# Layer 1 of a four-layer graph network: the order of TensorE's instructions written out by hand, with the next pair's features and the half's end as steps inside it

## The chip, the cores and the metric

The kernel runs on one core of one Trainium2 chip. The metric is the device time of one execution in microseconds (us), smaller is better. Most executions of one kernel agree within 0.3%.

## The reference

x has the shape (8, 2048, 64); adj is a 2048 x 2048 matrix of zeros and ones. Four layers follow each other, each as `x = x + layer(relu(layernorm(x)))`. The change lies in layer 1, a graph attention:

```python
h = jnp.matmul(input, W)
s_src = jnp.matmul(h, a[:C, 0])
s_dst = jnp.matmul(h, a[C:, 0])
e = jax.nn.leaky_relu(s_src[:, :, None] + s_dst[:, None, :], negative_slope=0.2)
attention = jax.nn.softmax(jnp.where(adj > 0.5, e, NEG_INF), axis=2)
return jax.nn.elu(jnp.matmul(attention, h))
```

Layer 0 is a hypergraph attention with a gate, layer 2 three rounds of a product with adj and two small linear maps, layer 3 a graph convolution of order 3 whose weights depend on the node.

## The kernel before

**Tiling.** Batches are taken in pairs: NP = 4 pairs, each with 2 x 64 features on the 128 partitions and N = 2048 nodes along the free axis. All of adj (transposed, 16 tiles `aT[m]` of 128 x 2048) lies in SBUF from the end of layer 0 on.

**Layer 1** is the class `Layer1`. For each pair p there is first a part that prepares the nodes as neighbours, `neighbour_steps(p)`, a generator. It goes through four chunks c of 512 columns. For each it loads x from DRAM on SP's queue, normalizes (`norm_steps`, lines 714 to 727: a matmul for the mean, L719; a subtraction on VectorE, L720; a square on ScalarE, L721; a matmul for the variance, L724; Ln and Exp on ScalarE, L725 and L726; the product on VectorE, L727), and then, twice, makes features of 256 nodes: four matmuls into `ph` (L1302; two in the text, each of them two records in the trace), an Exp `vd` on ScalarE (L1303), a copy `sc` (L1304) and a product `hS` (L1305) on VectorE. At the end come two small Exps `wd` and `rs` (L1311, L1313), a transpose `pr` (L1315), its copy `rr` and a store of that row to DRAM. It yields at some places, and the caller decides what is placed between. `mean` and `var` share one bank of PSUM (tag `ln`), and `ph` has one (tag `h`).

Then `attend` runs twice per pair, once for each half `hf` of the columns (1024 of them). It loads `R`, two broadcast rows of scores (512 KB each, three buffers in rotation), and loops over the 16 tiles m of neighbours:

- on VectorE two instructions `pt` (L1370), one for each batch of the pair, make the weights of 128 neighbours x 1024 nodes; there are five `pt` buffers;
- on TensorE `features` (L1355) adds `hS` times `pt` into `o`: four matmuls in column tiles of 64, so that the two batches can run beside each other;
- on TensorE `sums` (L1361) adds `vd` times `pt` into `dn`: four matmuls in column tiles of 32. `dn` has one buffer, `o` two.

For even m features come first, for odd m sums, so that equal kinds of two tiles m stand next to each other.

After the loop comes the half's end: `ds` takes `dn` out of PSUM (L1377), two matmuls `prd` spread it over the partitions (L1381), ScalarE takes Ln and Exp (L1382, L1383), and VectorE makes the product `res` (L1385), a minimum (L1387), after an Exp on ScalarE (L1388) the ELU (L1389) and the sum with x (L1390). POOL's queue stores it as x2 in DRAM (L1391).

**What sets the order.** The text gives each instruction a priority, its place. A planner then plays the program through with its own idea of costs and, on each engine, takes the first instruction in the text's order that it thinks is ready. So the instructions of an engine may be sent in another order than the text's; within the engine's queue they then run in that order. `tc.keep_in_program_order(ins)` binds one instruction to its place in the text. Before, it is used in layer 0's end, for one table load, and in layer 3; nothing in layer 1's loop is bound. In the text, `run` calls `attend(p, 0)`, then all of `neighbours(p + 1)`, then `attend(p, 1)`.

Pair 0's neighbours are made during the end of layer 0: `layer0` takes the steps of the same generator, two for each (p, c) of its last loop from the eighth on (`next(next_, None)`), and what is left after that loop. There, R of the first half is not loaded but made by 16 matmuls `pb` (L1326) and four copies on ScalarE (L1327).

Of the kernel before, what the change touches and what calls it, by code (L numbers as in the profile page):

```python
# [8 lines left out]
FP = mybir.dt.float32  # L9
FR = mybir.dt.float32r  # L10
AF = mybir.ActivationFunctionType
OP = mybir.AluOpType
# [4 lines left out]
P = 128  # L17
B, N, F = 8, 2048, 64
E = 64
NP = B // 2  # L20
NT = N // P
# [596 lines left out]
HN = N // 2  # L618
# [3 lines left out]
class Kit:  # L622


    def __init__(self, tc, t, pool):
        nc = self.nc = tc.nc
        self.tc, self.t = tc, t
        self.ident = pool.tile([P, P], FP, name="ident_f")
        make_identity(nc, self.ident)
        self.ones = pool.tile([P, F], FP, name="ones_f")  # L630
        nc.vector.memset(self.ones, 1.0)
        self.avg = pool.tile([P, P], FP, name="avg_f")
        nc.vector.memset(self.avg, 0.0)
        for b2 in range(2):
            nc.vector.memset(self.avg[half(b2), half(b2)], 1.0 / F)
        self.eps = pool.tile([P, 1], FP, name="eps_f")
        nc.vector.memset(self.eps, EPS)

        self.wide = pool.tile([P, P], FP, name="wide")
        nc.vector.memset(self.wide, 0.0)  # L640
        for q in range(4):
            nc.vector.memset(self.wide[32 * q : 32 * q + 32, half(q % 2)], 1.0 / 32)
        self.W1x = pool.tile([P, P + 4], FP, name="W1x")
        for k in ("W1v", "W1e", "W2", "Wvc", "Wec", "cb"):
            setattr(self, k, pool.tile([P, P], FP, name=f"{k}_f"))
        for k in ("b1", "b2c", "ivc", "b1c"):
            setattr(self, k, pool.tile([P, 1], FP, name=f"{k}_f"))

        self.bad = pool.tile([P, 7 + NT * NCW], FP, name="bad")
        nc.vector.memset(self.bad, 0.0)  # L650
# [35 lines left out]
    def layer2_weights(self, pool, ps):  # L686
# [21 lines left out]
        mm(pw, r, self.W1e, start=True, stop=True)  # L708
        nc.vector.tensor_copy(self.cb, pw)

    def use_ln_exp(self):
        self.tc.keep_in_program_order(self.nc.scalar.preload_act_table_set(LN_EXP))

    def norm_steps(self, dst, src, mean, var, xc, q):

        nc, mm = self.nc, self.nc.tensor.matmul
        n = dst.shape[-1] // CW
        for c in range(n):
            mm(mean[:, cols(c)], self.avg, src[:, cols(c)], start=True, stop=True)  # L719
        nc.vector.tensor_sub(xc, src, mean)  # L720
        nc.scalar.activation(q, xc, AF.Square)  # L721
        yield
        for c in range(n):
            mm(var[:, cols(c)], self.avg, q[:, cols(c)], start=True, stop=True)  # L724
        nc.scalar.activation(q, var, AF.Ln, bias=self.eps)  # L725
        nc.scalar.activation(q, q, AF.Exp, scale=-0.5)  # L726
        nc.vector.scalar_tensor_tensor(dst, xc, 0.0, q, op0=OP.max, op1=OP.mult)  # L727
        yield
# [525 lines left out]
class Layer1:  # L1254
# [14 lines left out]
        self.R = l1.enter_context(tc.tile_pool(name="l1_R", bufs=2, side="right", reuse_waits="tile"))  # L1269
        self.ps = ps = l1.enter_context(tc.tile_pool(name="l1_ps", bufs=1, space=PSUM, reuse_waits="tile"))  # L1270

    def neighbours(self, p):

        return [r for r in self.neighbour_steps(p)][-1]

    def neighbour_steps(self, p):


        kit, sb, ps, Wx = self.kit, self.sb, self.ps, self.kit.W1x
        tc, nc = kit.tc, kit.nc  # L1280
        mm = nc.tensor.matmul
        x1_dram, r_dram = self.x1_dram, self.r_dram
        hS = (self.sb2 if p % 2 else sb).tile([P, NT, P], FP, tag="hS", name="hS", bufs=1)
        vd = sb.tile([P, NT, 2], FP, tag="vd", name="vd")
        sc = sb.tile([P, NT, 4], FP, tag="sc", name="sc", bufs=1)
        wd = sb.tile([P, NT, 2], FP, tag="wd", name="wd")
        for c in range(NCW):
            x = sb.tile([P, CW], FP, tag="x", name="x1", bufs=1)
            nc.sync.dma_start(out=x, in_=x1_dram[p, :, cols(c)])
            mean = ps.tile([P, CW], FP, tag="ln", name="mean")  # L1290
            var = ps.tile([P, CW], FP, tag="ln", name="var")
            xc = sb.tile([P, CW], FP, tag="xc", name="xc")
            q = sb.tile([P, CW], FP, tag="q", name="q", bufs=1)
            hn = xc
            for _ in kit.norm_steps(hn, x, mean, var, xc, q):
                yield
            for g in range(2):
                ms = slice(4 * c + 2 * g, 4 * c + 2 * g + 2)
                ph = ps.tile([P, 2, P + 4], FP, tag="h", name="ph")
                for k in range(2):  # L1300
                    j = 2 * g + k
                    mm(ph[:, k, :], hn[:, j * P : (j + 1) * P], Wx, start=True, stop=True)  # L1302
                nc.scalar.activation(vd[:, ms, :], ph[:, :, P : P + 2], AF.Exp, scale=0.2)  # L1303
                nc.vector.tensor_copy(sc[:, ms, :], ph[:, :, P:])  # L1304
                nc.vector.tensor_tensor(  # L1305
                    hS[:, ms, :].rearrange("p t (b f) -> p t b f", b=2),
                    ph[:, :, 0:P].rearrange("p t (b f) -> p t b f", b=2),
                    vd[:, ms, :, None].to_broadcast([P, 2, 2, F]), op=OP.mult,
                )
        yield  # L1310
        nc.scalar.activation(wd, sc[:, :, 0:2], AF.Exp, scale=0.8)  # L1311
        rs = sb.tile([P, 2, NT], FP, tag="rs", name="rs", bufs=1)
        nc.scalar.activation(rs, sc[:, :, 2:4].rearrange("p t b -> p b t"), AF.Exp, scale=-0.8)  # L1313
        pr = ps.tile([2 * NT, P], FP, tag="h", name="pr")
        nc.tensor.transpose(pr, rs.rearrange("p b t -> p (b t)"), kit.ident)  # L1315
        rr = sb.tile([2 * NT, P], FP, tag="rr", name="rr", bufs=1)
        nc.vector.tensor_copy(rr, pr)
        nc.sync.dma_start(out=r_dram[p].rearrange("b (t n) -> (b t) n", n=P), in_=rr)
        self.first = [self.scores(p, 0, b2) for b2 in range(2)] if p == 0 else None

        for b2, r in enumerate(self.first or ()):
            for k in range(2):
                pb = ps.tile([P, 4, P], FP, tag=("ln", "h")[k], name="pb1")
                for j in range(4):
                    one = rs[:, b2, 4 * k + j : 4 * k + j + 1]
                    mm(pb[:, j, :], one.to_broadcast([P, P]), kit.ident, start=True, stop=True)  # L1326
                nc.scalar.copy(r[:, cols(k)], pb.rearrange("p k n -> p (k n)"))  # L1327
        yield hS, vd, wd
# [7 lines left out]
        self.kit.nc.sync.dma_start(out=r, in_=self.r_dram[p, b2 : b2 + 1, cols(hf, HN)].to_broadcast([P, HN]))  # L1336
        return r

    def attend(self, aT, p, hS, vd, wd, hf):
        kit, sb, ps, wide = self.kit, self.sb2, self.ps2, self.kit.wide  # L1340
        tc, nc = kit.tc, kit.nc
        mm = nc.tensor.matmul
        x1_dram, x2_dram, r_dram = self.x1_dram, self.x2_dram, self.r_dram
        s = cols(hf, HN)
        R = self.first or [self.scores(p, hf, b2) for b2 in range(2)]
        self.first = None
        x = sb.tile([P, HN], FP, tag="xr", name="xr", bufs=1)
        nc.sync.dma_start(out=x, in_=x1_dram[p, :, s])
        o = ps.tile([P, HN], FP, tag="o", name="o")
        dn = ps.tile([P, CW], FP, tag="dn", name="dn", bufs=1)  # L1350

# [14 lines left out]
        for m in range(NT):  # L1366
            pts = []
            for b2 in range(2):
# [2 lines left out]
                    pt, R[b2], wd[:, m, b2 : b2 + 1], aT[m][:, s].bitcast(FP), op0=OP.max, op1=OP.mult  # L1371
                )
                pts.append(pt)
            for f in (features, sums)[:: -1 if m % 2 else 1]:
                f(m, pts)
        ds = self.sb.tile([P, CW], FP, tag="xc", name="ds")
        nc.vector.tensor_scalar_max(ds, dn, 1e-30)  # L1377
        den = sb.tile([P, HN], FP, tag="den", name="den", bufs=1)
        for k in range(2):
            pr = ps.tile([P, CW], FP, tag="r", name="prd", bufs=1)  # L1380
            mm(pr, wide[half(k), :], ds[half(k), :], start=True, stop=True)  # L1381
            nc.scalar.activation(den[:, cols(k)], pr, AF.Ln)  # L1382
        nc.scalar.activation(den, den, AF.Exp, scale=-1.0)  # L1383
        r = sb.tile([P, HN], FP, tag="res", name="res", bufs=1)
        nc.vector.tensor_mul(r, o, den)  # L1385
        e = sb.tile([P, HN], FP, tag="den", name="e", bufs=1)
        nc.vector.tensor_scalar(e, r, 0.0, None, op0=OP.min)  # L1387
        nc.scalar.activation(e, e, AF.Exp)  # L1388
        nc.vector.scalar_tensor_tensor(e, e, -1.0, r, op0=OP.add, op1=OP.max)  # L1389
        nc.vector.tensor_add(x, x, e)  # L1390
        nc.gpsimd.dma_start(out=x2_dram[p, :, s], in_=x)  # L1391

    def run(self, aT, now):

        kit, l1 = self.kit, self.l1
        tc, nc = kit.tc, kit.nc
        self.pt = l1.enter_context(tc.tile_pool(name="att_pt", bufs=5, reuse_waits="tile"))
        self.sb2 = sb = l1.enter_context(tc.tile_pool(name="att_sb", bufs=2, reuse_waits="tile"))
        self.ps2 = l1.enter_context(tc.tile_pool(name="att_ps", bufs=2, space=PSUM, reuse_waits="tile"))
        kit.use_ln_exp()  # L1400
        for p in range(NP):
            self.attend(aT, p, *now, 0)
            if p + 1 < NP:
                after = self.neighbours(p + 1)
            self.attend(aT, p, *now, 1)
            now = after
        l1.close()


# [282 lines left out]
```

The softmax here doesn't subtract the row's maximum and nothing guards it: scores larger than these inputs give would overflow.

## Time and profile before

| what | value |
|---|---|
| device time, median of 3 runs | 2194.04 us (2191.21 to 2198.37) |
| the profiled run | 2193.25 us, its span 2191.5 us |
| busy in the span: PE, PEld, DVE, ACT, POOL | 2095.4, 1156.9, 1217.6, 452.3, 298.8 us |
| layer 1, first `o` to last `dn`/`o` | about 538 to 991 us |
| in it: `o` L1355, 1024 records | 267.7 us busy |
| in it: `dn` L1361, 1024 records | 142.4 us busy |
| in it: `pt` L1370, 256 instructions | 319.1 us busy |
| one `pt` (128 x 1024) | 1280 ns, 1.22 us from start to start |
| one Exp on 128 x 1024 (L1388) | 1058 ns |

PE is TensorE's matmuls, PEld its weight loads, DVE is VectorE, ACT is ScalarE, POOL is GpSimd; SP issues DMAs. In a timeline, instructions of one kind that follow each other are one row: the start, the length, engine, line, operation, what is written from what, and after the x how many. For the price of such a group in a full queue the text takes the time from its start to the start of the next row, since the modelled lengths overlap a little.

### The profile page before, as it was taken

How to read it: one execution, taken by the hardware profiler on the slowest of the kernel's cores; microseconds unless marked ns; L12 is line 12 of the kernel's file. 1: busy time of each engine (PE TensorE's matmuls, PEld its weight loads, DVE VectorE, ACT ScalarE, POOL GpSimd, SP SyncE). 2: the span in 40 equal slices, each digit the busy share in tenths (PEclk: the TensorE clock that was granted, in tenths of full speed). 3: DMA queues.
4: the chain of work that ended last, by engine and by line, in shares of the span. 5: the costliest groups of instructions: out<-in, count | busy, mean ns of one | idle time of the engine just before them, and what ended most of it. 6: DMA issues, size and time to landing. Idle time of an engine off the chain costs nothing.

```text
span 2191.5 us, 23784 instructions
## 1 busy us (share of the span) xinstructions
PE 2095.4 (96%) x9164; PEld 1156.9 (53%) x9164; DVE 1217.6 (56%) x1890; ACT 452.3 (21%) x852; POOL 298.8 (14%) x416
## 2 busy tenths in 40 slices
PE   7999999888999999998999999999999999999997
PEld 4777656523222222225666546774557664576653
DVE  6575488867888787884223563116551236501265
ACT  4312244465111102002121111120111211112100
POOL 0211154401000000000110121101111011111022
PEclk9999799989999999999999999999999999999999
DMA  5665362155011101104210014000030100101000
GB/s 123 195 199 158 105 220 50 40 168 164 29 49 34 62 30 44 39 30 132 68 43 8 22 33 127 24 20 19 25 101 6 44 10 21 42 1 34 12 19 12
DMA packets 86154, 140.26 MB, mean 64 GB/s; under 512 B 33040, under 2 KB 33296, under 8 KB 83792
## 3 DMA queue, kind: packets, MB, share of 16 engines
q1 hardware_dynamic: 67984, 88.05, 13.7%
q0 software_dynamic: 18048, 50.60, 7.7%
q8 instruction: 74, 1.21, 0.2%
q14 instruction: 48, 0.39, 0.1%
HBM read 107.89 MB, written 30.74 MB: 63 GB/s over the span
## 4 chain that ended last, share of the span: by engine, by line
PE 63%; issue 16%; DVE 7%; DMA 5%; POOL 4%; ACT 3%; POOLq 0%; DVEq 0%; SPq 0%; ACTq 0%
PE acc L1486 19%; PE o L1355 11%; PE u L1564 7%; PE dn L1361 6%; DMA raw<-in_adjT 3%; PE acc L913 2%; PE var L724 2%; PE pgs L1141 2%; PE py L1459 2%; PE mean L719 2%; PE acc L1515 1%; DVE ex L1139 1%; DMA at<-in_adjT 1%; POOL fold L1583 1%; PE ph L1302 1%
## 5 line engine op out<-in xcount | busy, mean ns | idle before, releaser
L1486 PE MATMUL acc<-aT,hi 128*128 128x512 f32 x960 | 401.2, 418 | 0.0
L1486 PE MATMUL acc<-aT,lo 128*128 128x512 f32 x960 | 388.2, 405 | 0.0
L1355 PE MATMUL o<-pt,hS 128*64 128x512 f32 x1024 | 267.7, 605 | 5.8 <-DVE pt L1370 5.8
L1370 DVE SCALAR_TENSOR_TENSOR pt<-R,wd,aT 128x1024 f32<-128x1024 f32 x192 | 239.1, 1280 | 38.6 <-PE dn L1361 21.6
L1564 PE MATMUL u<-W3f,y 64*128 64x512 f32 x1024 | 258.2, 592 | 0.0
L1572 DVE TENSOR_TENSOR pr<-u,embf 128x512 f32<-128x512 f32 x256 | 171.4, 687 | 123.0 <-PE u L1564 111.0
L1486 PEld LDWEIGHTS acc<-aT,hi 128*128 128x128 f32 x960 | 180.6, 188 | 61.8 <-issue 23.2
L1486 PEld LDWEIGHTS acc<-aT,lo 128*128 128x128 f32 x960 | 180.7, 188 | 51.2 <-issue 13.6
L1564 PEld LDWEIGHTS u<-W3f,y 64*128 64x128 f32 x1024 | 104.1, 187 | 124.8 <-issue 124.8
L1355 PEld LDWEIGHTS o<-pt,hS 128*64 128x64 f32 x1024 | 70.5, 137 | 187.1 <-issue 173.5
L1564 PE MATMUL u<-W3f,v 64*128 64x512 f32 x512 | 146.4, 617 | 0.0
L1361 PE MATMUL dn<-pt,vd 128*32 128x512 f32 x1024 | 142.4, 599 | 0.0
L913 PE MATMUL acc<-at,Y 128*128 128x512 f32 x512 | 137.4, 414 | 2.3 <-DVE ev L922 2.3
L1486 PE MATMUL acc<-aTl,lo 128*128 128x512 f32 x320 | 127.6, 399 | 5.6 <-DVE lo L1463 3.9
L1486 PE MATMUL acc<-aTl,hi 128*128 128x512 f32 x320 | 126.9, 397 | 4.7 <-ACT hi L1467 4.7
L1583 POOL TENSOR_TENSOR fold<-fold 128x256 f32<-128x256 f32 x64 | 47.6, 743 | 555.9 <-DVE fold L1582 555.9
L913 PEld LDWEIGHTS acc<-at,Y 128*128 128x128 f32 x512 | 95.9, 196 | 26.5 <-issue 4.9
L1466 DVE TENSOR_TENSOR yb<-py,cb_f 128x512 f32<-128x512 f32 x32 | 22.1, 690 | 156.1 <-PE py L1459 156.1
L721 ACT ACTIVATE q<-xc 128x512 f32<-128x512 f32 (+1 forms) x56 | 38.7, 691 | 264.8 <-DVE xc L720 253.4
L1576 DVE TENSOR_TENSOR pr<-pr 128x512 f32<-128x512 f32 x128 | 88.1, 688 | 2.2
L1442 DVE SCALAR_TENSOR_TENSOR raw<-raw 128x512 f32<-128x512 f32 x64 | 47.8, 750 | 72.4 <-DMA raw<-in_adjT 72.1
L1479 DVE TENSOR_TENSOR lo<-tp,hi 128x512 fp32r<-128x512 f32 x32 | 22.2, 692 | 117.5 <-ACT hi L1478 117.5
(278 smaller groups left out, 2717.7 us busy)
## 6 DMA issues: line engine op xcount, KB each, us to landing
at<-in_adjT POOLq DMA_DIRECT2D x32, 512.0 KB, 4.6
raw<-in_adjT SPq DMA_DIRECT2D x64, 256.0 KB, 3.3
aT<-in_adjT POOLq DMA_DIRECT2D x12, 1024.0 KB, 6.4
R<-r_dram SPq DMA_DIRECT2D x14, 512.0 KB, 3.6
hi_dram<-hi SPq DMA_DIRECT2D x16, 264.0 KB, 2.5
lo_dram<-lo SPq DMA_DIRECT2D x16, 264.0 KB, 3.6
hhi<-hi_dram POOLq DMA_DIRECT2D x16, 264.0 KB, 3.1
hlo<-lo_dram POOLq DMA_DIRECT2D x16, 264.0 KB, 3.1
```

What stands on the lines that cost most here:

```text
L719: mm(mean[:, cols(c)], self.avg, src[:, cols(c)], start=True, stop=True)
L724: mm(var[:, cols(c)], self.avg, q[:, cols(c)], start=True, stop=True)
L913: mm(acc[p], Y[h][:, m, p, :], at[:, k, :], start=m + h == 0, stop=m == NT - 1 and h == 1)
L1355: mm(o[half(b2), cols(k)], hS[:, m, half(b2)], pts[b2][:, cols(k)], start=m == 0, stop=m == NT - 1)
L1361: mm(dn[q : q + 32, :], vd[:, m, b2 : b2 + 1].to_broadcast([P, 32]), pts[b2][:, cols(k)], start=m == 0, stop=m == NT - 1, tile_position=(0 ...
L1370: nc.vector.scalar_tensor_tensor(pt, R[b2], wd[:, m, b2 : b2 + 1], aT[m][:, s].bitcast(FP), op0=OP.max, op1=OP.mult)
L1442: nc.vector.scalar_tensor_tensor(a, a, 0.5, a, op0=OP.is_gt, op1=OP.not_equal, accum_out=kit.bad[:, k : k + 1])
L1486: mm(acc, part[:, m % 4, :], aT[m][:, cols(c)], start=start, stop=m == NT - 1 and part is y[m // 4][1])
L1564: one = mm(u[h].rearrange("p d o -> p (d o)"), src[half(h), :], W3[half(h), kk, cols(w)], start=kk == 0, stop=kk == 2,)
L1572: nc.vector.tensor_tensor(a, u[h], emb[:, i, 8 * w : 8 * w + 8, None].to_broadcast([P, 8, F]), op=OP.mult)
L1576: nc.vector.tensor_add(pr[h], pr[h], a)
L1583: nc.gpsimd.tensor_add(fold[:, :, 0:2, :], fold[:, :, 0:2, :], fold[:, :, 2:4, :])
```

## The change

- A switch `kit.strict`, on from the start of layer 1's `run` to its end. While it is on, every matmul of `features`, `sums`, the totals `prd`, the norms and `ph`, and the transpose `pr`, is bound to its place in the text (`Kit.mm`).
- `attend` calls `between(m)` between the first and the second of features and sums of each m. There, in `run`, the next pair's neighbour steps are taken, by a pattern of (2, 0, 1, 0, 1) steps over five m, one fewer at m = 0 and 20, with m counted over both halves (0 to 31). So they begin at m = 0 of the first half and the 17th and last is taken at m = 22.
- The generator yields more often: after the mean, after the variance, and after each of the two feature groups, so 17 steps instead of 10 up to the result.
- The half's end is cut into two functions that run in the next half, after the first of features and sums: the first total `prd` at m = 1, the second and all that follows it at m = 2. Only `ds` stays at the end of its own half. After the last half both run at once.
- The minimum on VectorE (L1387) becomes a Relu with scale -1 on ScalarE, and the Exp after it gets the scale -1.

```diff
+    def mm(self, *args, **kw):
+        one = self.nc.tensor.matmul(*args, **kw)
+        if self.strict:
+            self.tc.keep_in_program_order(one)
...
     def norm_steps(self, dst, src, mean, var, xc, q):
-        nc, mm = self.nc, self.nc.tensor.matmul
+        nc, mm = self.nc, self.mm
...
     def neighbour_steps(self, p):
-        mm = nc.tensor.matmul
+        nc, mm = kit.nc, kit.mm
...
             for g in range(2):
+                if g:
+                    yield
                 ms = slice(4 * c + 2 * g, 4 * c + 2 * g + 2)
...
-        yield
+            yield
         nc.scalar.activation(wd, sc[:, :, 0:2], AF.Exp, scale=0.8)
...
-        nc.tensor.transpose(pr, rs.rearrange("p b t -> p (b t)"), kit.ident)
+        one = nc.tensor.transpose(pr, rs.rearrange("p b t -> p (b t)"), kit.ident)
+        if kit.strict:
+            kit.tc.keep_in_program_order(one)
...
-    def attend(self, aT, p, hS, vd, wd, hf):
+    def attend(self, aT, p, hS, vd, wd, hf, between):
...
-            for f in (features, sums)[:: -1 if m % 2 else 1]:
-                f(m, pts)
+            order = (features, sums)[:: -1 if m % 2 else 1]
+            order[0](m, pts)
+            between(m)
+            order[1](m, pts)
         ds = self.sb.tile([P, CW], FP, tag="xc", name="ds")
         nc.vector.tensor_scalar_max(ds, dn, 1e-30)
         den = sb.tile([P, HN], FP, tag="den", name="den", bufs=1)
-        for k in range(2):
+
+        def total(k):
             pr = ps.tile([P, CW], FP, tag="r", name="prd", bufs=1)
             mm(pr, wide[half(k), :], ds[half(k), :], start=True, stop=True)
             nc.scalar.activation(den[:, cols(k)], pr, AF.Ln)
...
+        def end():
+            total(1)
+            nc.scalar.activation(den, den, AF.Exp, scale=-1.0)
+            r = sb.tile([P, HN], FP, tag="res", name="res", bufs=1)
+            nc.vector.tensor_mul(r, o, den)
+            e = sb.tile([P, HN], FP, tag="den", name="e", bufs=1)
+            nc.scalar.activation(e, r, AF.Relu, scale=-1.0)
+            nc.scalar.activation(e, e, AF.Exp, scale=-1.0)
...
+        return [lambda: total(0), end]
...
     def run(self, aT, now):
         kit.use_ln_exp()
+        kit.strict = True
+        ends = []
         for p in range(NP):
-            self.attend(aT, p, *now, 0)
-            if p + 1 < NP:
-                after = self.neighbours(p + 1)
-            self.attend(aT, p, *now, 1)
-            now = after
+            steps = self.neighbour_steps(p + 1) if p + 1 < NP else iter(())
+            after = []
+            def between(m):
+                if m % NT and ends:
+                    ends.pop(0)()
+                for _ in range((2, 0, 1, 0, 1)[m % 5] - (m % 20 == 0)):
+                    after.append(next(steps, None))
+            for hf in range(2):
+                ends = self.attend(aT, p, *now, hf, lambda m: between(hf * NT + m))
+            after.extend(steps)
+            now = next((r for r in after if r), None)
+        for e in ends:
+            e()
+        kit.strict = False
```

More of the change, by code (lines that the diff above doesn't have):

```diff
@@ L626, in __init__ @@
         nc = self.nc = tc.nc
-        self.tc, self.t = tc, t
+        self.tc, self.t, self.strict = tc, t, False
         self.ident = pool.tile([P, P], FP, name="ident_f")
@@ L1270, in __init__ @@
         self.ps = ps = l1.enter_context(tc.tile_pool(name="l1_ps", bufs=1, space=PSUM, reuse_waits="tile"))
-    def neighbours(self, p):
-        return [r for r in self.neighbour_steps(p)][-1]
     def neighbour_steps(self, p):
         kit, sb, ps, Wx = self.kit, self.sb, self.ps, self.kit.W1x
-        tc, nc = kit.tc, kit.nc
-        mm = nc.tensor.matmul
+        nc, mm = kit.nc, kit.mm
         x1_dram, r_dram = self.x1_dram, self.r_dram
@@ L1337, in scores @@
         return r
-    def attend(self, aT, p, hS, vd, wd, hf):
+    def attend(self, aT, p, hS, vd, wd, hf, between):
         kit, sb, ps, wide = self.kit, self.sb2, self.ps2, self.kit.wide
-        tc, nc = kit.tc, kit.nc
-        mm = nc.tensor.matmul
-        x1_dram, x2_dram, r_dram = self.x1_dram, self.x2_dram, self.r_dram
+        nc, mm = kit.nc, kit.mm
         s = cols(hf, HN)
@@ L1347, in attend @@
         x = sb.tile([P, HN], FP, tag="xr", name="xr", bufs=1)
-        nc.sync.dma_start(out=x, in_=x1_dram[p, :, s])
+        nc.sync.dma_start(out=x, in_=self.x1_dram[p, :, s])
         o = ps.tile([P, HN], FP, tag="o", name="o")
@@ L1382, in attend @@
             nc.scalar.activation(den[:, cols(k)], pr, AF.Ln)
[L1383 to L1391, printed above, removed]
+        def end():
[6 more added lines that the diff above has]
+            nc.scalar.activation(e, e, AF.Exp, scale=-1.0)
+            nc.vector.scalar_tensor_tensor(e, e, -1.0, r, op0=OP.add, op1=OP.max)
+            nc.vector.tensor_add(x, x, e)
+            nc.gpsimd.dma_start(out=self.x2_dram[p, :, s], in_=x)
+        return [lambda: total(0), end]
     def run(self, aT, now):
```

## The prediction

> **What bounds the kernel now.** I went from the page to the stretch of layer 1, and inside it from engine totals to the order of TensorE's own instructions. First the table of windows, one row for layer 0's last part, one for layer 1 and one for the change to layer 2 (columns: length, then busy time of PE, PEld, DVE, ACT, POOL, granted clock, DMA share, GB/s):
>
> ```profile
> 464.00:522.00 58.00, 51.61 (x158) 19.73 (x157) 36.21 (x62) 37.90 (x54) 5.43 (x10) 0.91 0.53 161
> ...
> 538.00:991.00 453.00, 451.14 (x2223) 122.48 (x2223) 374.61 (x366) 51.26 (x95) 3.75 (x7) 1.00 0.13 43
> 991.00:1005.00 14.00, 7.09 (x16) 3.41 (x17) 5.81 (x7) 5.26 (x8) 0.53 (x1) 0.66 0.20 70
> ```
>
> Layer 1 is 453 us of 2191.5. TensorE is busy for 451 of them at full clock; VectorE has 374.6, so 78 us of room. TensorE sets the pace, but "busy" isn't "useful". The timeline of TensorE at the first half end shows why (start, length, then the group):
>
> ```profile
> 580.27 1.92 PE L1361 MATMUL dn<-pt,vd 128*32 128x512 f32 x16
> 582.13 1.94 PE L1355 MATMUL o<-pt,hS 128*64 128x512 f32 x8
> ...
> 587.10 1.12 PE L724 MATMUL var<-q,avg_f 128*128 128x512 f32 x2
> 588.16 1.93 PE L1355 MATMUL o<-pt,hS 128*64 128x512 f32 x6
> 590.02 1.04 PE L1361 MATMUL dn<-pt,vd 128*32 128x512 f32 x2
> 591.00 1.12 PE L719 MATMUL mean<-x,avg_f 128*128 128x512 f32 x2
> 592.05 1.06 PE L1361 MATMUL dn<-pt,vd 128*32 128x512 f32 x8
> 593.04 0.72 PE L1302 MATMUL ph<-W1x,xc 128*128 128x132 f32 x4
> 593.69 1.06 PE L1361 MATMUL dn<-pt,vd 128*32 128x512 f32 x6
> 594.68 1.08 PE L1355 MATMUL o<-pt,hS 128*64 128x512 f32 x4
> 595.69 1.13 PE L724 MATMUL var<-q,avg_f 128*128 128x512 f32 x2
> 596.75 1.07 PE L1355 MATMUL o<-pt,hS 128*64 128x512 f32 x2
> ```
>
> Each matmul of the text is two records, so one m-step is x8 of `o` (features) and x8 of `dn` (sums). Undisturbed, two steps run as x16 + x16. From start to next start over the stage, an `o` x16 takes 3.585 us and a `dn` x16 1.842. But `o` x6 takes 1.86, `o` x2 0.99, `dn` x8 0.99, `dn` x6 0.99, `dn` x2 0.98. An x8 of `o` cut into x6 and x2 costs 2.85 instead of 1.79; a `dn` x8 cut in two 1.96 instead of 0.92. The column tiles run beside each other only while their partners are next in the queue, and each cut wastes about 1 us. No wait shows it: PE is busy.
>
> The waits in layer 1 agree that TensorE waits for next to nothing, and VectorE for TensorE:
>
> ```profile
> DVE pt L1370 <- PE dn L1361: 25.6, 45, 3.4
> ...
> DVE res L1385 <- ACT den L1383: 14.3, 8, 5.7
> DVE pt L1370 <- PE o L1355: 13.4, 42, 1.2
> ...
> DVE pt L1370 <- DMA R<-r_dram: 7.3, 7, 2.0
> ...
> PE o L1355 <- DVE pt L1370: 5.8, 1, 5.8
> ```
>
> The last line is the start of the layer, which stays.
>
> **What the Trainium skill says.** "TensorEngine Tiling (Array Packing)", Key Properties: changing the tiling mode drains TensorE. The trace agrees: every short group carries some 0.15 us over its share (`o` x8 1.87 against 3.585/2). "TensorE: Matmul & The Clock Gate", Architectural detail: only weight loads are pulled ahead on TensorE, VectorE and ScalarE are strictly in order; so a bound step that waits holds all matmuls behind it. Before, a wait was filled with other matmuls, so no run here shows that cost. "ScalarE: Activation LUTs", Table sets: relu is in every set, so the new Relu needs no table load; the trace has no Relu, but only one table load in this stage.
>
> **The change, part by part.**
>
> 1. *Text order on TensorE.* The sum of a stage without cuts: 64 x (3.585 + 1.842) = 347.3, and 0.2 for the two half groups at the ends: 347.5. Now `o` and `dn` take 397.4 from 538.04 to 991.2, by start-to-start times. Of the 49.9 over, 2.3 is the first group's wait for its `pt`s (4.17 instead of 1.87), which stays. That leaves 47.6 to go. The guests between features and sums keep their price, as a boundary is there anyway: mean 12 x 1.055, var 12 x 1.007, ph 24 x 0.623, pr 3 x 0.22, totals 16 x 1.05. One mean, run at 529.5 in layer 0 now, comes into the stage: +1.06. Net **-46.5**; a stage of 407 us.
>
> 2. *VectorE as supplier.* Five `pt` buffers, two held by the m-step in work, three ahead: VectorE can be away 5.43 - 1.22 = 4.2 us before features of m+2 wait. At a half boundary it loses R's wait 1.0 (7.3/7), ds 0.6, res + e + add 3.45 (start to start), the wait for den 1.2 ((14.3 - 5.7)/7): 6.3; in first halves also sub, norm and sc+hS: 1.6. TensorE meanwhile spends 2.1 on totals, 3 x 0.27 of slack (2.71 of PE against 2 x 1.22 of DVE per m-step) and in first halves mean, var, ph 2.7. Net lag 2.3 to 3.4, under 4.2: nothing, if its queue is in the best order. I allow one `pt` (1.22) behind the wrong instruction at each of 7 boundaries: **+8**; bounds 0 and 20 (three such). min on VectorE (0.61 x 8) becomes Relu on ScalarE (1.06 x 8); ScalarE has 51 us of work in 453, so nothing, except in the tail.
>
> 3. *Steps' own waits.* Behind each bound step stand all features and sums, and behind those VectorE for `pt` buffers. Gaps in TensorE's own work: mean to var 5.4 to 6.5 us, var to ph 5.4 to 6.5, ph to ph 3.58 or, at m = 4/5 and 14/15, only 1.85 (two sums). After a ph, vd, sc and hS took 0.8 us where VectorE was free (600.46 to 601.27 after its end) and 3.5 where it was in other work (593.69 to 597.17). I take 0.5 for each of 6 narrow gaps: **+3**; bounds 0 and 10 (6 x 1.65). Moved DMAs: 4 x-loads, rr and the R loads on SP keep slack: a step's x is asked for a whole chunk (five m-steps, 14 us) ahead at 2.9 us to landing; rr is stored at m = 22, ten m-steps before R is used. xr waits on POOL's store of the half before, now some 3 us later, and is needed half a half later.
>
> 4. *Layer 0's end.* Pair 0 uses the same generator, unbound: 17 steps instead of 10, so with two per iteration its end moves from the 12th to the 16th (p, c). A front is 2.93 us there (454.97 to 457.89), so up to 4 x 2.93 = 12 late if R (pb 4.05 us, four copies of 0.59) came last; but VectorE is in layer 0's sums until 536.7 anyway, and finer steps may fill the 3.5 us wait at 473.9. I take **+1**, bounds -6 and +12.
>
> 5. *Tail.* Two totals, Ln, Exp, res, then e: the 14 us to layer 2 stay. Relu for min is +0.4 on e, but layer 2's subtraction no longer stands behind min (0.6): 0, bounds -1 and +1.
>
> Sum: -46.5 + 8 + 3 + 1 = -34.5. The span goes from 2191.5 to 2157.0. The profiled run's time is 2193.25, 0.8 under the median 2194.04 and well inside the runs (2191.21 to 2198.37); so the forecast is 2193.25 - 34.5 = **2159 us**, 1.6% faster.
>
> **Rivals.**
> - *VectorE becomes the bound.* Its 374.6 us less 5 for min, plus 7.3 for R and the 27 us it waits on short chains (res 8.6, sc 8.7, mean 6.3, norm 3.2) is 404 against TensorE's 407: two full queues in turn lose to each other. If five buffers don't decouple them, 20 us more than the 11 of parts 2 and 3: 2179. For it: 92% of 407 is VectorE work. Against: at 671 VectorE had filled all buffers and waited 3.39 us.
> - *Slower: each bound step waits one `pt`.* One mechanism, on the 48 steps (mean, var, ph) whose data pass through VectorE: if each finds a `pt` queued ahead (1.28 us) that its gap doesn't hide, 48 x 1.28 = 61, and the time is 2193 - 46.5 + 61 + 1 = 2209. It is slower by more than 0.3% (6.6 us) from 52 us on, 1.1 us a step. Against: gaps of 3.6 to 6.5 us at 42 of the 48.
> - *Layer 0 gives it back in part:* the upper bound of part 4, 2170.
> - *The order doesn't hold the groups together* (guests still between the partners): no change, 2193. Against: x16 groups form wherever nothing comes between, and the guests' place in the text is a boundary.
>
> **How the numbers follow.** Forecast (2148 to 2169) 0.58; under it, with no waits and a better end of layer 0, 0.07; VectorE bound or layer 0 late (2170 to 2186) 0.22; no change 0.05; slower 0.08. All but the last two are faster by over 0.3%, about what a measurement of this kernel can tell from no change: faster 0.87. The 8-in-10 range takes the forecast and most of its neighbours: low is no waits at all with a slightly better layer 0 (2193.25 - 46.5 - 1 = 2146), high the VectorE rival plus a few us of layer 0: 2183.
>
> **What would show it.** In layer 1 all `o` and `dn` as x8 and x16, no x2 or x6; stage 415 to 420 us; ph, mean and var at boundaries only; PE idle before `o` on DVE `pt` under 2 us a boundary (part 2); PEld ph on hS under 1 us (part 3); the first `o` near 538 to 540 (part 4). Wrong if PE's idle time on `pt` passes 20 us, if steps wait over 1 us each, or if layers 2 and 3 change their length.

## The result and the profile after

The changed kernel takes 2162.93 us (median of 4 runs, 2158.33 to 2164.11); the kernel before 2195.39 (median of 4, 2191.21 to 2198.37). The ratio is 0.985, its 95% interval 0.9827 to 0.9872: 1.5% faster. The forecast was 2159.

The profiled run's span is 2160.7 us, 30.8 less than before. First the table of windows of the changed kernel, cut at the first `o`, at the last total `prd` and at the end:

```profile
536.00:956.40 420.40, 415.44 (x2225) 121.55 (x2226) 366.58 (x359) 59.63 (x102) 3.74 (x7) 1.00 0.14 46
956.40:2160.70 1204.30, 1165.44 (x4932) 731.66 (x4932) 463.55 (x811) 181.09 (x324) 167.57 (x241) 0.99 0.13 37
```

From the first `o` to the start of the last total, layer 1 took 453.15 us before (538.04 to 991.19) and 420.40 after: 32.7 less. It starts 2.0 earlier. What follows the last total takes 1204.3 instead of 1200.3 (991.19 to 2191.5), which gives 4.0 back. -32.7 - 2.0 + 4.0 is the -30.8 of the span, up to rounding.

The timeline of TensorE in the changed kernel, where pair 0 gives way to pair 1. All matmuls called through the helper `Kit.mm` now have its line, L713, so go by the tiles:

```profile
644.28 1.12 PE L713 MATMUL mean<-x,avg_f 128*128 128x512 f32 x2
645.34 1.92 PE L713 MATMUL dn<-pt,vd 128*32 128x512 f32 x16
647.19 1.12 PE L713 MATMUL prd<-ds,wide 64*128 64x512 f32 x2
648.24 3.65 PE L713 MATMUL o<-pt,hS 128*64 128x512 f32 x16
651.83 1.12 PE L713 MATMUL prd<-ds,wide 64*128 64x512 f32 x2
652.88 1.13 PE L713 MATMUL var<-q,avg_f 128*128 128x512 f32 x2
653.93 1.92 PE L713 MATMUL dn<-pt,vd 128*32 128x512 f32 x16
655.79 4.03 PE L713 MATMUL o<-pt,hS 128*64 128x512 f32 x16
659.75 0.72 PE L713 MATMUL ph<-W1x,xc 128*128 128x132 f32 x4
660.39 1.90 PE L713 MATMUL dn<-pt,vd 128*32 128x512 f32 x10
663.62 1.06 PE L713 MATMUL dn<-pt,vd 128*32 128x512 f32 x6 [1.32 <-DVE pt L1375]
```

Guests (means, variances, `ph`, totals) stand between whole groups of 16, and no x2 and x6 of cut groups are left. The last two rows are no cut: no guest stands between them. TensorE ran out of `pt` after ten records of `dn`. These 16 records take 4.2 us from start to start instead of 1.85. So the new limit is a wait, for VectorE. The waits of the changed kernel in layer 1:

```profile
DVE pt L1375 <- PE dn L713: 17.9, 27, 1.3
...
DVE pt L1375 <- PE o L713: 9.4, 27, 1.0
...
PE o L713 <- DVE pt L1375: 5.2, 3, 4.1
DVE pt L1375 <- DMA R<-r_dram: 5.0, 5, 1.2
...
DVE res L1396 <- ACT den L1394: 4.0, 2, 2.0
...
PE dn L713 <- DVE pt L1375: 2.7, 2, 1.3
```

VectorE still waits for TensorE most of the time, but TensorE now waits for `pt` in the middle of the layer too. The table of waits counts only idle time; a wait inside a group of overlapping matmuls shows as a longer row, such as the `o` x16 of 4.03. By starts, `o` and `dn` take 364.1 us after against 397.4 before. Whole groups would be about 348. Of the rest, 2.9 is the first group's, which takes 4.73 us instead of 1.87. It comes after a wait of 4.06 us for the first `pt`, and from 537.2 to 540.6 the granted clock (1.00 is full speed) is 0.50. Another 13.0 are waits for `pt` inside the layer (3.1 in the first half of pairs 1 and 2 each, 1.2 in the second half of pairs 0, 1 and 2 each, 1.6 in each half of pair 3); the expectations below count them as 12.4.

### The profile page after: what moved, and what is told of

It is laid out like the page before. It is cut to its first block, busy times and chain, and to the rows that moved or that the text cites. A ratio compares the mean times of both kernels' runs of the same rounds, so it can differ in the third digit from the quotient of the medians.

```text
span 2160.7 us, 23805 instructions
## 1 busy us (share of the span) xinstructions
PE 2056.3 (95%) x9164; PEld 1156.7 (54%) x9164; DVE 1211.0 (56%) x1882; ACT 461.1 (21%) x860; POOL 297.4 (14%) x416
## 4 chain that ended last, share of the span: by engine, by line
PE 61%; issue 16%; DVE 8%; DMA 6%; POOL 4%; ACT 3%; POOLq 0%; DVEq 0%; SPq 0%; ACTq 0%
PE acc L1514 19%; PE o L713 10%; PE u L1592 7%; PE dn L713 5%; DMA raw<-in_adjT 3%; PE acc L919 2%; PE var L713 2%; PE pgs L1147 2%; PE py L1487 2%; PE mean L713 2%; PE acc L1543 1%; DVE pt L1375 1%; DMA at<-in_adjT 1%; DVE ex L1145 1%; POOL fold L1611 1%
## 5 line engine op out<-in xcount | busy, mean ns | idle before, releaser
L713 PE MATMUL o<-pt,hS 128*64 128x512 f32 x1024 | 243.5, 602 | 5.7 <-DVE pt L1375 5.2
L713 PEld LDWEIGHTS o<-pt,hS 128*64 128x64 f32 x1024 | 70.3, 137 | 169.8 <-issue 149.0
L713 PE MATMUL dn<-pt,vd 128*32 128x512 f32 x1024 | 125.3, 598 | 2.7 <-DVE pt L1375 2.7
L919 PEld LDWEIGHTS acc<-at,Y 128*128 128x128 f32 x512 | 93.5, 191 | 24.3 <-issue 4.2
L1375 DVE SCALAR_TENSOR_TENSOR pt<-R,wd,aTl 128x1024 f32<-128x1024 f32 x64 | 80.0, 1282 | 10.3 <-PE dn L713 7.4
```

Of the source, the lines that this page charges most:

```text
L713: one = self.nc.tensor.matmul(*args, **kw)
L919: mm(acc[p], Y[h][:, m, p, :], at[:, k, :], start=m + h == 0, stop=m == NT - 1 and h == 1)
L1375: nc.vector.scalar_tensor_tensor(pt, R[b2], wd[:, m, b2 : b2 + 1], aT[m][:, s].bitcast(FP), op0=OP.max, op1=OP.mult)
```

## The experiments

Since layer 0 and the layers after differ by a few us between executions of one kernel, each run is read by its stage, from the first `o` to the last total. The changed kernel run once more gives 419.8:

> The changed kernel once more, for how much each stretch varies from execution to execution: stage 420 within 1 us; layer 0 and layers 2 and 3 within some 4 us of the first profile.

Measured: 2162.11 us, stage 419.80. The waits inside the layer are those of the first profile within 0.02 us; the first group is 0.5 shorter. What follows the stage took 1203.5. So a stage can be compared to within a microsecond, and the parts around it cannot.

### A guest inside the group

```diff
-            order[0](m, pts)
-            between(m)
+            order[0](m, pts, between)
             order[1](m, pts)
```

`features` and `sums` call the handed-in `between(m)` after the first of their four matmuls.

> The changed kernel with the guests (steps and ends) after the first of the four matmuls of the first group instead of after the group: 51 places with a cut. Theory (a cut group costs about 1 us): 51 x 1.02 = 52 us more TensorE time in layer 1, of which up to 12 is time in which it waits for pt now: stage 460 to 472, time 2203 to 2215. Rival (cuts cost little, the gain came from moving ends and steps): within 8 us of 2163.

Measured: 2197.05 us, stage 458.69. The timeline of TensorE in this run:

```profile
602.61 1.90 PE L713 MATMUL dn<-pt,vd 128*32 128x512 f32 x10
604.45 1.12 PE L713 MATMUL prd<-ds,wide 64*128 64x512 f32 x2
605.50 1.13 PE L713 MATMUL var<-q,avg_f 128*128 128x512 f32 x2
606.55 1.06 PE L713 MATMUL dn<-pt,vd 128*32 128x512 f32 x6
607.54 2.79 PE L713 MATMUL o<-pt,hS 128*64 128x512 f32 x10
610.26 1.12 PE L713 MATMUL prd<-ds,wide 64*128 64x512 f32 x2
611.31 1.93 PE L713 MATMUL o<-pt,hS 128*64 128x512 f32 x6
```

The `dn` of two m-steps takes 1.84 + 0.99 = 2.83 us in two pieces instead of 1.85, the `o` 2.72 + 1.86 = 4.58 instead of 3.585. A cut is 1.0 us. 51 of them would be 51 us; `o` and `dn` took 37.4 more than in the changed kernel, because the slower TensorE hardly waits for `pt` any more (13.0 of waits to lose). The stage is 1.3 us under the expected range. The gain is given back with the cuts alone, with all instructions the same: the mechanism that the prediction rests on.

Not every cut costs so much, as the pieces in the kernel before show. There `o` x2 takes 1.00 us and x4 1.01, x6 1.86 and x8 1.87, x12 2.73 and x16 3.58. So two matmuls of the text (x4), one for each batch, take as long as one alone. A cut through such a pair costs 1.0; a cut between two pairs, as in x4 and x12, costs 0.15. For `dn`, x2, x6 and x8 take 0.98, 0.99 and 0.99: there a whole m-step runs together.

### The new text without the binding

```diff
-        kit.strict = True
+        kit.strict = False
```

> The changed kernel with its steps and half ends where the change puts them in the text, but nothing in layer 1 bound. Theory (the binding keeps the groups whole): the planner cuts them again, o and dn as x2 and x6, layer 1 longer than the changed kernel's 420 us by 15 to 35, so 2178 to 2198 us. Rival (the place in the text is enough): few cuts, stage 415 to 425, time within 5 us of 2163.

Measured: 2175.73 us, stage 427.31; both theories missed in part. The groups are cut again, but much less: 10 `o` x2 and 8 `dn` x2, where the kernel before has 30 and 13. By the stage alone, the place of the steps and ends in the text brings 25.8 of the 32.7 us, the binding 6.9. But the stage leaves out what happens at its start. The timeline of that run:

```profile
536.25 1.13 PE L713 MATMUL var<-q,avg_f 128*128 128x512 f32 x2 [1.57 <-ACT q L727]
538.43 2.05 PE L713 MATMUL mean<-x,avg_f 128*128 128x512 f32 x2 [1.05 <-DMA x<-xd]
...
542.14 1.12 PE L713 MATMUL var<-q,avg_f 128*128 128x512 f32 x2 [0.79 <-ACT q L727]
545.08 2.04 PE L713 MATMUL mean<-x,avg_f 128*128 128x512 f32 x2 [1.82 <-DMA x<-xd]
547.06 1.60 PE L713 MATMUL o<-pt,hS 128*64 128x512 f32 x2
```

Unbound, the planner puts the next pair's first steps ahead of the first features. They wait for each other and for DMAs, and VectorE's first `pt` comes 7 us later too (541.68 instead of 534.67, though part of this is that run's later layer 0: its output part began 4.1 us later). The first `o` comes 103.2 us after the beginning of layer 0's output part, instead of 96.3. Three means, two variances and a `ph` stand ahead of the first `o`, 5.7 us of guests that the changed kernel has inside its stage, so the stage alone is too kind to the unbound kernel. From the beginning of that output part to the last total the three kernels take 550.8 us (before), 530.5 (unbound) and 516.7 (changed): the place brings 20 of 34, the binding 14. `o` and `dn` alone, with 397.4, 376.9 and 364.1, say nearly the same. Both figures hold for five `pt` buffers, where the bound kernel loses 13.0 us to waits for `pt` and the unbound one some 3; the unbound kernel with six was not run.

### The binding without the new text

The kernel before with `Kit.mm` and `strict` alone, neighbours in one block between the halves, ends at their own half.

> The kernel before with layer 1's TensorE instructions bound to its own text order: neighbours in one block between the halves, ends at their own half. Theory: no cut groups (-46), but TensorE now waits in the block: some 5 us per chunk (subtraction 0.7, square 0.6, Ln 0.7, Exp 0.6, product 0.7, vd and hS 0.8, less what VectorE has queued ahead) x 12 = 60, and 1 to 1.5 us at each of 8 ends, so 2210 to 2235 us, slower than before. Rival (binding alone brings the gain): 2155 to 2170.

Measured: 2262.51 us, stage 524.79, 72 us longer than before. The waits of TensorE in that run, and its windows (a stretch of plain attention, then the block of steps):

```profile
PE ph L712 <- DVE xc L732: 31.1, 12, 3.6
PE var L712 <- ACT q L726: 17.8, 12, 1.5
PE ph L712 <- DVE hS L1310: 10.8, 12, 1.0
```

```profile
534.00:576.00 42.00, 41.76 (x228) 11.37 (x230) 37.48 (x32) 0.00 (x0) 0.00 (x0) 0.93 0.12 39
576.00:634.00 58.00, 36.32 (x93) 13.97 (x89) 21.66 (x36) 12.63 (x26) 0.54 (x1) 0.57 0.15 46
```

The waits are 60 us, as expected (31.1 + 17.8 + 10.8). What the sum missed is the clock. In this first block of steps, with waits of 0.9 to 3.6 us one behind the other, it is 0.57 in the mean, and a mean, 1.12 us long otherwise, takes 2.07. The low clock begins at 584, after two waits of no more than 0.16 and 0.69 us for the totals, and lasts until 635. Binding is only good where the text has enough work between a step and the next that needs it.

### The half's end back at its own half

```diff
-                ends = self.attend(aT, p, *now, hf, lambda m: between(hf * NT + m))
+                for e in self.attend(aT, p, *now, hf, lambda m: between(hf * NT + m)):
+                    e()
```

> The changed kernel, bound as there, with each half's end at its own end again. Theory (a bound matmul that waits holds all behind it): at each of 7 boundaries the second total waits 0.7 for ScalarE, features(15) and features(0) no longer stand together (0.15), and VectorE's burst comes when it has also R and ds to wait for, 1 to 2 us: stage 8 to 20 us longer than 420, 2170 to 2185. Rival (moving the ends is worth nothing beside the whole groups): stage within 3 us of 420.

Measured: 2157.50 us, stage 423.32, 2.9 more than the changed kernel's and just inside the rival's 3. But the ends are not without effect; two effects nearly cancel. The second total of each end waits 0.7 us for ScalarE, `ds` is waited for 2.8 in all, and features no longer stand together at the boundary. Against that, by the starts of its groups TensorE waits only 2.1 us for `pt` inside the layer, where it waits 13.0 in the changed kernel. And at three of the seven boundaries something else follows the waits:

```profile
691.60 1.12 PE L713 MATMUL prd<-ds,wide 64*128 64x512 f32 x2 [0.79 <-DVE ds L1384]
693.41 1.58 PE L713 MATMUL prd<-ds,wide 64*128 64x512 f32 x2 [0.69 <-ACT den L1390]
694.91 3.13 PE L713 MATMUL o<-pt,hS 128*64 128x512 f32 x8
```

From 693.95 to 697.36 the granted clock is 0.50, and the `o` x8 takes 3.06 us from start to start instead of 1.87, with no wait in it. The three boundaries lose 4.1 us in `o` this way. The time itself is under the changed kernel's, since the stage began at 526.4 in this run, which is layer 0's doing.

### VectorE as supplier: three edits

Six `pt` buffers instead of five (`bufs=6`):

> The changed kernel with six pt buffers instead of five. Theory (the 12.4 us that TensorE waits inside layer 1 are VectorE's bursts at half boundaries, longer than the lead of three buffers): one more buffer is 1.22 us more of lead at each of 10 waits (three of 1.2, two of 1.0 to 1.5, two of 2.9 in parts): most go, stage 410 to 414, 2153 to 2158. Rival (the waits come from the steps' own chains): stage within 2 us of 420.

The half's end in four parts, at m = 1, 2, 4 and 7:

```diff
-                if m % NT and ends:
+                if m % NT in (1, 2, 4, 7) and ends:
                     ends.pop(0)()
...
-        return [lambda: total(0), end]
+        return [lambda: total(0), end, elu, add]
```

> The changed kernel with the half's end in four parts, at m = 1, 2, 4 and 7 (Relu and Exp at 4, the ELU and the sum at 7) instead of 1 and 2. Theory: VectorE's burst of 3.5 us is spread over 14 us and TensorE's waits fall from 12.4 to 2 to 6: stage 410 to 414, 2153 to 2158. Rival (VectorE is simply too full; the sum of its work counts, not where it stands): within 2 us of 420.

Both:

> Six pt buffers and the half's end in four parts together. Theory (with six buffers TensorE already waits only at the start and at the last totals, 3.2 us): nothing is left to gain, stage 407 to 410, within 4 us of the six buffers alone at 2145. Rival (spreading gives something more): under 2140.

| kernel | median us | ratio to before (95%) | stage us |
|---|---|---|---|
| changed | 2162.93 | 0.985 (0.9827 to 0.9872) | 420.4 |
| six buffers | 2144.79 | 0.9773 (0.9736 to 0.981) | 408.5 |
| end in four parts | 2148.32 | 0.9792 (0.9749 to 0.9834) | 413.0 |
| both | 2144.48 | 0.9752 (0.9733 to 0.9772) | 407.2 |

The same place as above, in the timeline of the run with six buffers:

```profile
655.19 1.92 PE L713 MATMUL dn<-pt,vd 128*32 128x512 f32 x16
657.04 3.65 PE L713 MATMUL o<-pt,hS 128*64 128x512 f32 x16
660.63 0.72 PE L713 MATMUL ph<-W1x,xc 128*128 128x132 f32 x4
661.28 1.92 PE L713 MATMUL dn<-pt,vd 128*32 128x512 f32 x16
663.40 0.69 PE L713 MATMUL ph<-W1x,xc 128*128 128x132 f32 x4 [0.20 <-DVE hS L1308]
```

The `dn` that took 4.2 us is whole, at 1.92, and 11.6 of the 13.0 us of waits are gone; TensorE's order is the same as in the changed kernel. It was VectorE's burst against the lead that five buffers give. The stage, 408.5, is better than the expected 410 to 414. Spreading the end over four places left 6.1 us of waits, and its stage lies in the expected range. The six-buffer kernel beats both kernels and is the one to keep; spreading on top of it adds nothing that shows. Its stage is within 2 us of the 407 of TensorE's own work. Of the 18 us in the medians the stage has 12; the rest lies in the layers after it (1196.6 us in this profile, 1204.3 in the changed kernel's), where the edit leaves the instructions and their order as they are, and isn't put down to it. Two waits of TensorE in layer 2, `acc` for `hi`, make up 4.0 of that difference (5.9 us in the changed kernel, 1.9 here, 4.7 before); why they vary stays open.

The minimum on VectorE again:

```diff
-            nc.scalar.activation(e, r, AF.Relu, scale=-1.0)
-            nc.scalar.activation(e, e, AF.Exp, scale=-1.0)
+            nc.vector.tensor_scalar(e, r, 0.0, None, op0=OP.min)
+            nc.scalar.activation(e, e, AF.Exp)
```

> The changed kernel with the minimum on VectorE again instead of the Relu on ScalarE. Theory: 0.6 us more of VectorE work at each of seven half boundaries, where TensorE waits for pt: stage 0 to 5 us longer than 420, 2163 to 2168. Rival (ScalarE's longer chain, Relu 1.06 before Exp, sets when VectorE can go on): stage 1 to 5 us shorter.

Measured: 2158.69 us, stage 424.38, 4.0 longer: 0.6 us at each of 7 boundaries is 4.2. The time is lower than the changed kernel's only because the stage began at 531.4 instead of 536.0 and what follows it was 3.1 shorter in this run.

### Layer 0's end

> The changed kernel with pair 0's generator in layer 0 yielding as before (10 steps instead of 17). Theory: layer 1's first o starts at about 538 as in the kernel before, 2 us later than the changed kernel's 536, and nothing else moves. Rival (the earlier start is run-to-run): starts at 536.

Measured: 2165.55 us, stage 419.61, first `o` at 540.5. Alone that proves nothing, since layer 0's output part begins (first `pf` from `iv`) anywhere from 435 to 446 us. So the length from there to the first `o` is what counts, and the extra yields were put into the kernel before alone:

```diff
             for g in range(2):
+                if g:
+                    yield
...
-        yield
+            yield
         nc.scalar.activation(wd, sc[:, :, 0:2], AF.Exp, scale=0.8)
```

> The kernel before with nothing but the generator's extra yields, which only layer 0's end sees. Theory (finer steps shorten layer 0's end): from its first pf to layer 1's first o 93 to 96 us, where the kernel before shows 97.6; layer 1 stays at about 453; 2189 to 2194. Rival (the difference is run to run): 97 to 101.

Measured: 2192.84 us; from the first `pf` at 437.05 to the first `o` at 530.43 it is 93.4 us. All profiles together, without the unbound run: coarse steps 97.6 (before), 98.8 (bound only), 101.2 (this layer 0 undone); fine steps 96.3 and 94.3 (changed, twice), 93.7, 94.3, 93.7, 93.5, 93.4, 93.4 and 90.6. They don't overlap. The finer steps shorten layer 0's end by about 5 us (means 99.2 and 93.7); by which waits was not traced. Layer 1 itself was 456.2 in this run, 3 us more than before, and what follows it 4.0 more, so the time hardly moved.

## Why the prediction was right, point by point

**The number** is nearer than its parts. In the profiles the stage missed by +2.8 us (-32.7 instead of -35.5), its start by -3.0 (-2.0 instead of +1), and what follows by +4.0. The first two cancel, which is luck; the -46.5 that decides the forecast is not.

**What bounds layer 1** was right: a TensorE that is busy with cut groups. The price of a cut, read as about 1 us from the trace of before, is 1.0 when made on purpose. The reading of 0.15 us a short group was about twice too high: 2 x 1.87 - 3.585 = 0.15 is what one more group costs, so an `o` x8 is 0.08 over its half of an x16. That this is the drain which the cited page names is not shown; the trace has only the sum.

**Part 1 (-46.5).** The sum held: with the waits taken away by six buffers the stage is 408.5, of which 3.2 are the excess of the first group and the last totals' wait. Two small readings were off: a whole `dn` x16 takes 1.853, not 1.842, 0.7 us over the stage; and the 2.3 us of the first group are for the most part a clock of 0.50, not a wait in the group. The part's heading, text order on TensorE, gives the binding too much: the place in the text brings 20 of 34 us unbound, the binding the other 14. Neither works as a rule: binding the old text costs 72 us.

**Part 2 (+8)** was 13.0. The step that was mis-sized is the lead, "VectorE can be away 5.43 - 1.22 = 4.2 us". An `o` or `dn` group of 16 reads the `pt`s of two m-steps, so the buffers don't come free evenly. Taken in turn, a buffer of every second `pt` is let go of by TensorE 3.0 us before the `pt` that takes its place is needed, in the traces of before and after alike. Less the 1.22 that a `pt` takes, that is a lead of 1.8 us (an estimate from those starts and ends); with six buffers it is at least 4.05. The net lag of 2.3 to 3.4 that the part worked out is under 4.2, but over 1.8.

Pair 3, which has no steps beside it, shows the burst of an end alone (VectorE, and the last row TensorE):

```profile
870.50 1.28 DVE L1375 SCALAR_TENSOR_TENSOR pt<-R,wd,aT 128x1024 f32<-128x1024 f32 x1 [1.30 <-PE dn L713]
871.70 1.22 DVE L1396 TENSOR_TENSOR res<-o,den 128x1024 f32<-128x1024 f32 x1
872.83 2.48 DVE L1375 SCALAR_TENSOR_TENSOR pt<-R,wd,aT 128x1024 f32<-128x1024 f32 x2
875.22 1.22 DVE L1400 SCALAR_TENSOR_TENSOR e<-e,res 128x1024 f32<-128x1024 f32 x1
876.36 1.28 DVE L1375 SCALAR_TENSOR_TENSOR pt<-R,wd,aT 128x1024 f32<-128x1024 f32 x1
877.55 1.22 DVE L1401 TENSOR_TENSOR xr<-xr,e 128x1024 f32<-128x1024 f32 x1
878.69 8.46 DVE L1375 SCALAR_TENSOR_TENSOR pt<-R,wd,aT 128x1024 f32<-128x1024 f32 x7
880.03 1.93 PE L713 MATMUL o<-pt,hS 128*64 128x512 f32 x6 [0.56 <-DVE pt L1375]
```

At 870.50 VectorE has just waited for a buffer, so it is as far ahead as it can be. After that it waits for nothing, yet `res`, `e` and `xr` between the `pt`s are enough: the `o` x16 with that last row takes 5.2 us instead of 3.58. In the second halves of pairs 0 to 2 the next pair's `sc` and `hS` stand in the burst too, which the part counted in first halves only.

The allowance itself, a `pt` behind the wrong instruction, isn't what came. The nearest thing to it is in the first halves of pairs 1 and 2, where `res` waits 2.01 us for ScalarE ahead of the next `pt`:

```profile
654.70 1.23 DVE L1396 TENSOR_TENSOR res<-o,den 128x1024 f32<-128x1024 f32 x1 [2.01 <-ACT den L1394]
```

But the buffer of that next `pt` came free only at 654.99, so no `pt` was held up during that wait; at most the 1.23 us of `res` itself moved behind that moment. And with six buffers `res` waits 2.01 us there too. In all `res` waits 4.0 us for `den`, less than the 7 x 1.2 of the part.

**Part 3 (+3)** was 0: no step waits for its own data in the changed kernel: from the first `o` to the last total, TensorE's listed waits are for `pt` alone. A narrow gap waits 0.2 us, twice, once VectorE is further ahead, in the run with six buffers. "TensorE: Matmul & The Clock Gate" says in Architectural detail that TensorE's queue can pull weight loads ahead of matmuls. That a waiting matmul holds the matmuls behind it the trace of before couldn't show; the bound-only run agrees, with 60 us of waits that nothing filled.

**Part 4 (+1)** had the wrong sign: -1.3 in this pair of profiles (97.6 to 96.3 after the first `pf`), about -5 over all. Its fear, "up to 4 x 2.93 = 12 late if R (pb 4.05 us, four copies of 0.59) came last", didn't come true, and "finer steps may fill the 3.5 us wait" got too little weight: the runs show that finer steps help, not that they help by filling waits.

**Part 5 (0)** held: from the last total to layer 2's first `py` it was 10.98 us and is 11.28. Relu for min was priced at nothing; with five buffers it saves 4.0. It brought no table load: both profiles have 11.

**The rest of the miss** is the 4.0 us after layer 1 in the profile, one of the prediction's own signs of being wrong. In all 13 profiles, that of before and that of the bound-only kernel among them, this stretch was between 1196 and 1206 us, and the change's two profiles, 1204.3 and 1203.5, lie inside, so it isn't put down to the change; what moves it stays open.

**The rivals.** VectorE as the bound was the nearest: present, at 13.0 us instead of 31. The slower one, a `pt` ahead of each bound step, didn't come, as the pattern leaves 3.6 to 6.5 us at most steps. Bound without such gaps there were waits of its size, 60 us, but behind the steps' own chains and the half's end, not behind a `pt`.

## What to carry to other kernels

A TensorE at 99% busy can be 10% slack: compare what a group costs whole and in pieces, from start to start, before looking for waits, since a matmul in column tiles that loses its partner takes as long as the pair and shows as busy. Give guests a place between whole groups in the text, far enough from the work that they need; bind the order after that, for the rest (14 of 34 us here), and don't bind a text in which one step follows on the heels of the one it needs. When TensorE gets faster, read the lead of the buffers that feed it from the trace, from the last use of a buffer to the first use of what fills it next, less the time to fill it, and take the smallest, not the count of buffers. Set it against the longest burst of other work on the supplier: here one more buffer took the smallest lead from 1.8 to 4.05 us and gave a third as much again as the change itself.

## What the runs showed of the hardware

- Column-tiled matmuls (512 elements long, f32) run together in sets: two of the text in tiles of 64 columns, four in tiles of 32. A part of a set takes as long as the whole (`o` x2 1.00 us, x4 1.01; `dn` x2 0.98, x8 0.99). A cut through a set costs 1.0 us, whatever stands in the cut; for `o`, a cut between two sets costs 0.15.
- Short waits between matmuls went with a low clock. In the first block of steps of the bound-only run, waits of 0.9 to 3.6 us one behind the other kept it at 0.57 in the mean of 58 us, and a mean took 2.07 us instead of 1.12. With each half's end back at its own half, two waits of some 0.7 us close together were followed by 3.4 us at 0.50 at three of seven boundaries. In the changed kernel, where the longest wait inside the layer is 1.3 us and stands alone, the mean clock of layer 1 was 1.00.
- Where no instruction differs, the stretch after layer 1 was 1204.3 us in the changed kernel and 1196.6 with six buffers, and layer 0's output part began at 439.7, 442.7 and 445.1 in the changed kernel, its repeat and the six-buffer kernel. Layer 1 repeated within 0.6 us (420.40 and 419.80).
